# First-layer statistics moved into the products, the bias read in four transfers, W2 in halves, the first merge on VectorE

## The chip, the cores and the metric

One core of one Trainium2 chip runs the whole program in a single launch. The metric is the device time of that launch in microseconds, the median over repeated executions. TensorE (PE), VectorE (DVE), ScalarE (ACT), GpSimd (POOL) and the queues of SyncE (SP) work side by side; 16 DMA engines move data between HBM and the on-chip memory SBUF. Everything is float32.

## The reference, cut to what matters

```
def _gn(v, G=32, eps=1e-5):                 # group norm over (batch, channels, positions of one group)
    B_, H_, W_, C_ = v.shape
    g = v.reshape(B_, H_, W_, G, C_ // G)
    m = jnp.mean(g, axis=(1, 2, 4), keepdims=True)
    s = jnp.var(g, axis=(1, 2, 4), keepdims=True)
    return ((g - m) / jnp.sqrt(s + eps)).reshape(v.shape)

def conv(x, z, W1, b1, ..., W2, b2, Wb1, ..., Wb2, bb2):   # sizes: s 32, b 32, C 64, L 256, K 3, H 128
    h = relu(layernorm(z @ W1 + b1))
    w = (h @ W2 + b2).reshape(B, L, CI, CO, K)              # a convolution weight for every (b, l)
    hb = relu(layernorm(z @ Wb1 + bb1))
    bias = (hb @ Wb2 + bb2).transpose(0, 2, 1)
    x_uf = stack([pad(x)[..., i:i + L] for i in range(K)], -1)
    return einsum('sbilk,bliok->sbol', x_uf, w) + bias[None]

x = x + conv(_gn(x), layer 0 parameters)
x = x + conv(_gn(x), layer 1 parameters)
```

Each of the two layers normalizes x by group (32 groups of 8 positions), makes its own convolution weights from z by a small network, applies them, and adds a bias and the residual. The group statistics need all of the batch and all channels.

## The kernel before, in words

The work is cut into 128 chunks, numbered v = 0 to 127; 0 to 63 belong to layer 0 and 64 to 127 to layer 1. Chunk v is half h = v % 2 of the output channels of unit u = v // 2, and a unit is 4 batches and a quarter (64) of the positions. One iteration of the main loop, for chunk v, does this on TensorE: a first tile of weights of chunk v (`make`, L705 and L706: `h @ W2` for 8 output channels into PSUM, tiles `pg`, three buffers), then `products(v - 1)` (L760: the convolution of chunk v - 1 in four quarters, into PSUM tiles `pc`, two buffers), then eleven more weight tiles of chunk v. There are 672 matmul records in a chunk, 384 of the weights and 288 of the products.

- `take` (L717 on VectorE, L728 on ScalarE) adds b2 to a weight tile and writes it to `wall`, the weights of one chunk; `wall` has one buffer. One tile in three (kind 2) is split between VectorE and ScalarE; the others are VectorE's.
- In `products`, VectorE adds each quarter to the residual in `ring` (L772; `ring` has three slots, chunk v uses slot v % 3) and, in layer 0, takes the statistics of the result for layer 1 (`last_stats`, L369).
- GpSimd adds the bias to the residual ahead of time (`add_bias`, L653, from tile `bt`, one buffer) and normalizes the next unit's x (`normalize`, L691: one subtraction and one multiplication over half a unit, from `raw` into `xn`).
- SP issues nearly all DMAs in one queue, in program order: an issue that waits holds back all that follow it. In an iteration of the first 43 chunks these are: the store of the finished chunk (L658), `load_pieces` into `land` (L812), the next half unit into `raw` (L180), which waits until the subtraction of `normalize` has read the old one, the residual two chunks on (L202) and its bias (`load_bias`, L646). `load_bias` reads four rows of 8 KB and repeats each for 32 partitions, in one DMA of 1 MB.

The statistics of layer 0 are taken from x itself. Before chunk 0 only the first 11 of 32 groups are read (`first_phase`, loop over i; `needed` = 18 iterations give groups 0 to 8, which is what the first quarter of the positions needs); the other 21 groups are 168 pieces, four per chunk in chunks 1 to 42: `load_pieces(v)` at the start of iteration v fills `land`, and four VectorE instructions (`piece`, L819) placed among the weight tiles of the same iteration read it. Merges turn such statistics into mean and scale: `FirstMerge` before chunk 0, and eight `LaterMerge`s in later iterations, each with small DMAs through HBM (`turn`, `gather`, `root`; L445, L450, L471), small GpSimd operations (`mean`), a square root on ScalarE (L469) and a reciprocal on VectorE (L470). `Table.load` (L494) reads mean and scale back. `agenda(v)` says after which of the 12 weight tiles (todo[0] to todo[11]) each of these steps is issued.

## Time and profile before

| what | value |
|---|---|
| median of 3 runs | 4036.97 us (4033.2 to 4048.76) |
| the profiled execution, its own time | 4040.76 us |
| its span, first to last instruction | 4038.2 us |
| mean granted TensorE clock | 0.976 |

A profile is one execution. Busy times are sums for each engine; a wait is idle time of an engine just before an instruction, put down to what ended it. "x" is a count, times without a unit are microseconds, and a granted clock of 1.00 is 2.4 GHz, 0.50 is 1.2 GHz.

### The profile page before, as it was taken

What the parts mean: (1) busy time and instruction counts of PE and PEld (TensorE: products, weight loads), DVE (VectorE), ACT (ScalarE), POOL (GpSimd) and SP (SyncE); (2) the same over time, 40 slices, a digit from 0 to 9 for tenths busy, and PEclk for the clock granted to TensorE, in tenths of its full rate; (3) what the DMA queues carried; (4) which work ended last, traced back from release to release, by engine and by line L of the source; (5) the groups of instructions that cost most, each with busy time, mean ns of one, the idle gap of its engine ahead of it and who ended that gap; (6) DMA issues with size and microseconds to landing.
All of it is one profiled execution on the core that took longest, in us unless ns stands there. A gap on an engine that the chain in (4) does not pass through costs nothing.

```text
span 4038.2 us, 184843 instructions
## 1 busy us (share of the span) xinstructions
PE 3812.4 (94%) x86424; PEld 3699.1 (92%) x86424; DVE 2872.8 (71%) x3256; ACT 1263.0 (31%) x4330; POOL 1873.1 (46%) x713
## 2 busy tenths in 40 slices
PE   6888889989889989999999999999999999999999
PEld 4688889988888888999999999999999999999999
DVE  5766667766667666677677777777777777777776
ACT  4322222322233222333333233323332333333232
POOL 2144344444444444465454454555455454545453
PEclk8899999999999999999999999999999999999999
DMA  8844554545545454444446454555555555545453
GB/s 282 279 151 162 155 170 162 176 154 177 163 156 173 164 161 153 153 160 157 153 166 197 138 164 140 167 146 161 148 157 157 152 160 147 166 141 165 144 158 102
DMA packets 142861, 660.07 MB, mean 163 GB/s; under 512 B 45703, under 2 KB 51983, under 8 KB 76303
## 3 DMA queue, kind: packets, MB, share of 16 engines
q1 hardware_dynamic: 142095, 648.26, 51.0%
q8 instruction: 675, 11.06, 1.1%
q14 instruction: 91, 0.75, 0.1%
HBM read 499.16 MB, written 149.05 MB: 161 GB/s over the span
## 4 chain that ended last, share of the span: by engine, by line
PE 53%; DMA 1%; POOL 0%; issue 0%; ACT 0%; DVE 0%; SPq 0%; POOLq 0%; DVEq 0%
PE pg L705 35%; PE pc L760 14%; PE pg L706 4%; DMA bt<-bd 1%; DMA w2t<-in_L_conv_W_dram 1%; DMA land<-x 0%; POOL xn L691 0%; POOL ring L653 0%; ACT wall L728 0%; DVE wall L717 0%; ACT parts L390 0%; DVE ring L772 0%; DVE parts L369 0%; POOL four L454 0%; POOL found L455 0%
## 5 line engine op out<-in xcount | busy, mean ns | idle before, releaser
L705 PE MATMUL pg<-hT,w2t 128*64 128x128 f32 x24576 | 2779.2, 276 | 118.8 <-DVE wall L717 98.1
L705 PEld LDWEIGHTS pg<-hT,w2t 128*64 128x64 f32 x24576 | 2724.7, 139 | 156.2 <-DVE wall L717 112.5
L706 PE MATMUL pg<-hT,w2t 128*64 128x128 f32 x24576 | 2779.1, 276 | 3.5 <-issue 3.3
L706 PEld LDWEIGHTS pg<-hT,w2t 128*64 128x64 f32 x24576 | 2724.7, 139 | 7.6 <-issue 7.6
L717 DVE TENSOR_TENSOR wall<-pg,b 128x1024 f32<-128x1024 f32 (+1 forms) x1540 | 1871.8, 1218 | 600.3 <-PE pg L706 594.1
L728 ACT ACTIVATE wall<-pg,b 64x128 f32<-64x128 f32 x4064 | 1154.6, 468 | 2638.5 <-DVE wall L717 2638.3
L653 POOL TENSOR_TENSOR ring<-ring,bt 128x2048 f32<-128x2048 f32 x127 | 578.9, 4559 | 1934.0 <-DMA bt<-bd 1580.3
L760 PE MATMUL pc<-wall,xn 128*32 128x128 f32 (+1 forms) x36864 | 961.4, 264 | 60.4 <-DVE wall L717 31.6
L760 PEld LDWEIGHTS pc<-wall,xn 128*32 128x32 f32 x36864 | 925.4, 111 | 97.8 <-issue 89.8
L691 POOL TENSOR_TENSOR xn<-xn,tab 128x2112 f32<-128x2112 f32 x190 | 891.9, 4694 | 15.0
L772 DVE TENSOR_TENSOR ring<-pc,ring 128x512 f32<-128x512 f32 x512 | 353.9, 691 | 332.5 <-PE pc L760 224.5
L691 POOL TENSOR_TENSOR xn<-raw,tab 128x2112 f32<-128x2112 f32 x54 | 252.9, 4684 | 51.8 <-DMA raw<-in_xp_dram 51.5
L819 DVE BATCH_NORM_STATS2 first_parts<-land 128x6 f32<-128x512 f32 x168 | 114.4, 681 | 148.2 <-DMA land<-in_xg_dram 148.2
L369 DVE BATCH_NORM_STATS2 parts<-ring 128x6 f32<-128x256 f32 x512 | 191.9, 417 | 6.3
L209 DVE STREAM_TRANSPOSE xn<-raw 128x544 f32<-128x544 f32 (+1 forms) x128 | 138.9, 1104 | 0.0
L209 DVE STREAM_TRANSPOSE xn<-land 128x544 f32<-128x544 f32 (+1 forms) x128 | 138.8, 1103 | 0.0
L304 POOL TENSOR_TENSOR raw<-w2t,xn 128x256 f32<-128x256 f32 x16 | 10.3, 645 | 106.8 <-DVE xn L299 95.0
L328 PE MATMUL ph<-xn,wc 17*128 17x512 f32 x128 | 36.8, 776 | 16.3 <-DVE xn L294 6.8
L541 DVE BATCH_NORM_STATS2 first_parts<-ring 128x6 f32<-128x512 f32 x72 | 44.5, 676 | 9.3 <-DMA ring<-in_xg_dram 9.2
L328 PEld LDWEIGHTS ph<-xn,wc 17*128 17x128 f32 x128 | 10.1, 211 | 35.3 <-ACT xn L330 13.3
L330 ACT ACTIVATE xn<-ph,vec 128x1024 f32<-128x1024 f32 x32 | 36.1, 1199 | 5.4 <-DMA hd<-xn 3.2
L691 POOL TENSOR_TENSOR xn<-land,tab 128x2112 f32<-128x2112 f32 x8 | 37.6, 4702 | 0.0
(103 smaller groups left out, 366.3 us busy)
## 6 DMA issues: line engine op xcount, KB each, us to landing
bt<-bd SPq DMA_DIRECT2D x127, 1024.0 KB
ring<-in_xs_dram SPq DMA_DIRECT2D x64, 1024.0 KB
x<-ring SPq DMA_DIRECT2D x64, 1024.0 KB
ring<-x SPq DMA_DIRECT2D x64, 1024.0 KB
out_dram<-ring SPq DMA_DIRECT2D x64, 1024.0 KB
raw<-in_xp_dram SPq DMA_DIRECT2D x55, 1056.0 KB
land<-in_xg_dram SPq DMA_DIRECT2D x46, 1024.0 KB
raw<-x SPq DMA_DIRECT2D x128, 256.0 KB
```

The source lines that it names most:

```text
L209: nc.vector.transpose(xn[:, u % 2, k * NT // 2 + t, j0:j1], src)
L328: nc.tensor.matmul(p[:, r], self.w.wc[x, net], self.zq[x, net], start=True, stop=True)
L369: nc.vector.bn_stats(out, y[:, :, :, g * e : (g + 1) * e])
L653: nc.gpsimd.tensor_tensor(y, y, bts.pop(v).rearrange("p o (a m) -> p o a m", a=2), ALU.add)
L691: eng.tensor_tensor(o, i, tab[:, x, None, j0:j1].to_broadcast(list(o.shape)), op)
L705: nc.tensor.matmul(pg[0:C, k, :], w[:, k0 * C : (k0 + 1) * C], h0, start=True, stop=True)
L706: nc.tensor.matmul(pg[C:P, k, :], w[:, k1 * C : (k1 + 1) * C], h1, start=True, stop=True)
L717: nc.vector.tensor_tensor(place(rows, a), pg[rows].rearrange("p o (t m) -> p t m o", t=NT), b2[n][rows, kind, None, None, o0 : o0 + OG].to ...
L728: nc.scalar.activation(place(rows, a)[:, :, :, k], pg[rows, k].rearrange("p (t m) -> p t m", t=NT), AF.Identity, bias=b2[n][rows, kind, o0 ...
L760: nc.tensor.matmul(pc[t * S : (t + 1) * S, n0 - q * EB : n1 - q * EB, :], xn[:, u % 2, t, p, :], wall[:, t, a : a + (n1 - n0) * CH], start ...
L772: nc.vector.tensor_tensor(part, pc.rearrange("p (m a) o -> p a o m", a=2), part, ALU.add)
L819: nc.vector.bn_stats(first_parts[:, g, bg], lands[i % LAND])
```

## The change

1. The 168 pieces leave the weight tiles: `products(v)` now carries the four pieces of chunk v as its `turns` (two ahead of the first quarter's add, one behind it, one behind the second's), so data loaded in iteration v are read in iteration v + 1.
2. `load_bias` issues four DMAs of 32 partitions each instead of one of 128, for chunks up to 43; later chunks keep the one DMA.
3. `first_phase` ends after 18 iterations instead of 20. The four units of statistics that are left over (instead of two) run in iteration 1, and there the four kind-1 tiles go wholly to ScalarE. `FirstMerge` works on VectorE alone (`within`, `between`) and starts after iteration 17; the bias batches use other scratch memory.
4. In iteration 1 `products(0)` is issued ahead of the first weight tile of chunk 1.
5. The second half of W2 is loaded in four DMAs at the start; layer 1's W2 is loaded a half at a time, in iterations 63 and 64, instead of one eighth after each third tile of iterations 62 and 63.
6. `LaterMerge`: its DMAs and `Table.load` are issued by ScalarE's queue; one VectorE operation of `turn` becomes two small GpSimd operations; `gather` moves from the next iteration to todo[10] of its own, `mean` from todo[3] (behind `normalize` on GpSimd) to ahead of it, the square root from todo[10] to todo[5], the reciprocal to todo[6]. `Table.load` moves one iteration earlier, to todo[10].

The core of the diff:

```diff
@@ load_bias
-            nc.sync.dma_start(
-                out=bts[v].rearrange("p o l -> p (o l)"),
-                in_=bass.AP(src.tensor, src.offset, [src.ap[0], [0, S], src.ap[1]]),
-            )
+            to = bts[v].rearrange("p o l -> p (o l)")
+            n = 1 if v <= last_of[NQ - 1] + 1 else NT
+            for t in range(0, NT, n):
+                some = src[t : t + n]
+                nc.sync.dma_start(
+                    out=to[t * S : (t + n) * S],
+                    in_=bass.AP(some.tensor, some.offset, ([some.ap[0]] if n > 1 else []) + [[0, S], some.ap[1]]),
+                )
@@ products
-            turns = turns_of_half(u + 1, h, place_half(u + 1, h)) if UL <= u + 1 < U else []
+            if UL <= u + 1 < U:
+                turns = turns_of_half(u + 1, h, place_half(u + 1, h))
+            else:
+                turns = pieces_of(v)
@@ first_phase
-            for i in range(needed + 2):
+            for i in range(needed):
...
+                if i == needed - 1:
+                    merge = FirstMerge(first_parts.rearrange("p g b f -> p g (b f)")[:, 0:NG])
+                    table = Table(0)
+                    merge.within()
                 first_weights(i - (needed - 11))
-        rest = [lambda i=i, k=k: stats(i, range(k, k + 2)) for i in range(needed + 2, units) for k in (0, 2)]
+            merge.between()
+            biases(needed)
+            merge.root()
+            table.expand(nc.vector)
+            first_weights(11)
+            table.lay(table.spread(), [nc.vector.tensor_copy, nc.scalar.copy])
+            biases(needed + 1)
+            starting(0)
+            starting(1)
+        rest = [lambda i=i, k=k: stats(i, range(k, k + 2)) for i in range(needed, units) for k in (0, 2)]
@@ take
-                (add if alone else add_scalar)(slice(C, P), CH)
+                (add if v == 0 else add_scalar)(slice(C, P), CH)
-                add(slice(0, P), (3 * CH, 0)[kind])
+                (add_scalar if v == 1 and kind == 1 else add)(slice(0, P), (3 * CH, 0)[kind])
@@ agenda
-            w, r = divmod(v + 1, NH * BG)
+            w, r = divmod(v + 2, NH * BG)
-                todo[0].append(tables[w].load)
+                todo[10].append(tables[w].load)
+            for m in pending:
+                todo[0].append(m.mean)
+                todo[5].append(m.root)
+                todo[6].append(m.keep)
...
-            if v <= last_of[NQ - 1]:
-                for i in range(LAND):
-                    todo[8 + i if v == 1 else 5 + 2 * i].append(lambda i=(v - 1) * LAND + i: piece(i))
-            for m in pending:
-                todo[0].append(m.gather)
-                todo[3].append(m.mean)
-                todo[10].append(m.root)
+            n, i = divmod(v + 1, NH * UL)
+            if 0 < n < NL and i < NH:
+                for o in range(i * CH, (i + 1) * CH, OG):
+                    todo[1].append(lambda n=n, o=o: load_w2(n, o, o + OG))
...
                 todo[6].append(m.turn)
+                todo[7].append(m.send)
+                todo[10].append(m.gather)
@@ main loop
+            if v == 1:
+                products(0, cut_next)
             for k in range(len(order)):
                 pg = multiply(v, k)
-                if k == 0:
-                    products(v - 1, cut_next if v == 1 else None)
+                if k == 0 and v > 1:
+                    products(v - 1)
```

How the instructions stand on the engines, at the places that matter. First SP's queue in an iteration of about chunk 25, before (L658 stores a chunk, `land` takes the pieces, `raw` half a unit, `ring` a residual, `bt` its bias):

```order
L658 DMA x_12_84<-ring 128x2048
L812 DMA land<-in_xg_dram 128x2048
L180 DMA raw<-in_xp_dram 128x2112
L202 DMA ring<-in_xs_dram 128x2048
L646 DMA bt<-bd_160 128x1x2048
```

The same place with the change:

```order
L684 DMA x_12_84<-ring 128x2048
L834 DMA land<-in_xg_dram 128x2048
L180 DMA raw<-in_xp_dram 128x2112
L202 DMA ring<-in_xs_dram 128x2048
L672 DMA bt<-bd_160 32x2048 x4
```

Nothing moved in the queue; the bias, last in the row, is four DMAs of 32 partitions.

Second, VectorE from the products of one chunk (L772 adds a quarter, L369 takes layer 1's statistics) to the weight tiles behind them (L717), with the pieces (L819) before:

```order
L772 TENSOR_TENSOR ring<-pc,ring 128x64x8
L369 BN_STATS parts<-ring 128x6 x2
L772 TENSOR_TENSOR ring<-pc,ring 128x64x8
L717 TENSOR_TENSOR wall<-pg,b_0_219 128x128x8
L369 BN_STATS parts<-ring 128x6 x2
L717 TENSOR_TENSOR wall<-pg,b_0_219 64x128x8
L717 TENSOR_TENSOR wall<-pg,b_0_219 128x128x8 x2
L717 TENSOR_TENSOR wall<-pg,b_0_219 64x128x8
L717 TENSOR_TENSOR wall<-pg,b_0_219 128x128x8
L819 BN_STATS first_parts<-land 128x6
L717 TENSOR_TENSOR wall<-pg,b_0_219 128x128x8
```

The same stretch with the change, from the end of one chunk's tiles (L743 is now the add of `take`, L801 the add of a quarter, L843 a piece):

```order
L743 TENSOR_TENSOR wall<-pg,b_0_219 128x128x8 x2
L843 BN_STATS first_parts<-land 128x6 x2
L801 TENSOR_TENSOR ring<-pc,ring 128x64x8
L843 BN_STATS first_parts<-land 128x6
L369 BN_STATS parts<-ring 128x6 x2
L801 TENSOR_TENSOR ring<-pc,ring 128x64x8
L843 BN_STATS first_parts<-land 128x6
L369 BN_STATS parts<-ring 128x6 x2
L801 TENSOR_TENSOR ring<-pc,ring 128x64x8
L369 BN_STATS parts<-ring 128x6 x2
L801 TENSOR_TENSOR ring<-pc,ring 128x64x8
L743 TENSOR_TENSOR wall<-pg,b_0_219 128x128x8
```

The pieces left the tiles and stand between the adds of the first two quarters; the tiles behind follow each other with nothing between.

Third, SP's queue in iterations 62 and 63, where layer 1's W2 comes in (`w2t`), before:

```order
L136 DMA w2t<-in_L_conv_W_dram 128x1536
L202 DMA ring<-in_xs_dram 128x2048
L646 DMA bt<-bd_169 128x1x2048
L672 DMA xe_134<-rim 128x128
L136 DMA w2t<-in_L_conv_W_dram 128x1536 x3
L494 DMA spot<-tb_153 128x2x288
L658 DMA x_31_103<-ring 128x2048
L189 DMA land<-x_0_72 32x2x1024 x4
L136 DMA w2t<-in_L_conv_W_dram 128x1536
L202 DMA ring<-x_0_72 128x2048
L646 DMA bt<-bd_170 128x1x2048
L136 DMA w2t<-in_L_conv_W_dram 128x1536 x3
```

And with the change, iterations 63 and 64:

```order
L684 DMA x_31_103<-ring 128x2048
L189 DMA land<-x_0_72 32x2x1024 x4
L136 DMA w2t<-in_L_conv_W_dram 128x1536 x4
L202 DMA ring<-x_0_72 128x2048
L672 DMA bt<-bd_170 128x1x2048
L166 DMA edge<-xe_113 32x4x32 x2
L684 DMA x_31_103<-ring 128x2048
L189 DMA raw<-x_1_73 32x2x1024 x4
L136 DMA w2t<-in_L_conv_W_dram 128x1536 x4
L202 DMA ring<-x_0_72 128x2048
L672 DMA bt<-bd_170 128x1x2048
```

W2 is one iteration later, and all four DMAs of a half stand ahead of the residual and the bias; the table's load (`spot`) has left the queue.

## Rows read from the trace of the kernel before

**Rows 1.** The page: the span, and each engine's busy time with its share.

```profile
span 4038.2 us, 184843 instructions
PE 3812.4 (94%) x86424; PEld 3699.1 (92%) x86424; DVE 2872.8 (71%) x3256; ACT 1263.0 (31%) x4330; POOL 1873.1 (46%) x713
```

**Rows 2.** Windows: stretch, length, busy per engine, PEclk, DMA share, GB/s.

```profile
206.15:1643.72 1437.57, 1292.34 (x28897) 1254.85 (x28897) 976.02 (x1233) 416.97 (x1482) 625.86 (x213) 0.96 0.49 163
1674.60:2129.68 455.08, 453.39 (x10755) 448.29 (x10753) 326.02 (x390) 152.84 (x540) 232.70 (x80) 1.00 0.45 157
2158.04:2344.77 186.73, 173.86 (x4038) 170.84 (x4040) 135.94 (x146) 57.71 (x206) 93.64 (x47) 0.98 0.58 169
```

**Rows 3.** Chain that ended last, 1870 to 1935: start, length, what.

```profile
1875.16 7.18 PE pc L760 x288
...
1903.45 7.14 PE pc L760 x288
```

**Rows 4.** Waits, 206.15 to 1643.72: total, times, longest.

```profile
POOL ring L653 <- DMA bt<-bd: 579.4, 31, 21.9
...
DVE first_parts L819 <- DMA land<-in_xg_dram: 148.2, 34, 7.3
...
PE pg L705 <- DVE wall L717: 97.3, 50, 4.9
...
DVE found L470 <- ACT found L469: 27.5, 6, 6.8
```

**Rows 5.** Timeline, 401 to 436, of SP, POOL, DVE, PE (idle before).

```profile
401.06 0.53 SPq L646 DMA_DIRECT2D bt<-bd  x1
415.38 0.43 SPq L812 DMA_DIRECT2D land<-in_xg_dram  x1
425.50 4.51 POOL L653 TENSOR_TENSOR ring<-ring,bt 128x2048 f32<-128x2048 f32 x1 [20.34 <-DMA bt<-bd]
429.97 4.67 POOL L691 TENSOR_TENSOR xn<-raw,tab 128x2112 f32<-128x2112 f32 x1
429.85 0.69 DVE L819 BATCH_NORM_STATS2 first_parts<-land 128x6 f32<-128x512 f32 x1 [5.45 <-DMA land<-in_xg_dram]
431.72 0.47 PE L705 MATMUL pg<-hT,w2t 128*64 128x128 f32 x1 [3.35 <-DVE wall L717]
435.52 0.52 SPq L646 DMA_DIRECT2D bt<-bd  x1
```

**Rows 6.** Windows of 4 to 9 us, columns as in rows 2.

```profile
480.00:484.00 4.00, 4.00 (x160) 3.91 (x150) 3.19 (x7) 0.00 (x0) 0.00 (x0) 1.00 0.27 72
436.00:445.00 9.00, 9.00 (x228) 8.83 (x228) 5.57 (x8) 2.29 (x8) 3.54 (x2) 0.92 0.75 274
2873.00:2878.00 5.00, 5.00 (x97) 5.00 (x94) 3.42 (x4) 2.27 (x8) 4.92 (x2) 1.00 1.02 233
```

**Rows 7.** Timeline of SP, 2867 to 2873.

```profile
2867.80 3.74 SPq L189 DMA_DIRECT2D land<-x  x4
```

**Rows 8.** Groups by line and shape, DVE, 206.15 to 1643.72: busy, mean ns.

```profile
L369 DVE BATCH_NORM_STATS2 parts<-ring 128x6 f32<-128x256 f32 x344 | 129.1, 417 | 4.4
L772 DVE TENSOR_TENSOR ring<-pc,ring 128x512 f32<-128x512 f32 x172 | 118.9, 691 | 152.6 <-issue 84.4 <-PE pc L760 68.2
L819 DVE BATCH_NORM_STATS2 first_parts<-land 128x6 f32<-128x512 f32 x165 | 112.4, 681 | 148.2 <-DMA land<-in_xg_dram 148.2
```

**Rows 9.** Start: waits of PE, 140 to 182, and DVE's timeline.

```profile
PE pg L705 <- DMA w2t<-in_L_conv_W_dram: 4.9, 1, 4.9
...
157.92 2.47 DVE L541 BATCH_NORM_STATS2 first_parts<-ring 128x6 f32<-128x512 f32 x4
```

**Rows 10.** Timeline of POOL and ACT, 2195 to 2258.

```profile
2235.76 4.57 POOL L653 TENSOR_TENSOR ring<-ring,bt 128x2048 f32<-128x2048 f32 x1 [17.34 <-DMA bt<-bd]
...
2253.94 0.32 ACT L469 ACTIVATE found<-found,eps 8x32 f32<-8x32 f32 x1 [4.72 <-POOL found L455]
```

**Rows 11.** Waits of SP's queue, 206.15 to 1643.72.

```profile
SPq L494 <- DMA tb<-found: 28.7, 2, 15.1
```

More of the change, by code (lines that the diff above doesn't have):

```diff
@@ L264, in __init__ @@
             ht = [take(2 * BLK) for _ in range(2)]
-            self.bs = [take(BLK // 2).rearrange("p (t a m) -> p t a m", t=NT, a=2) for _ in range(4)]
             self.var = take(2 * NR * NR)
@@ L268, in __init__ @@
             self.ht = [[take(2 * BLK) for _ in range(2)], ht]
-            self.q = take(BLK)
+            self.q = raw[:, 2 * BLK : 3 * BLK]
             self.zq = take(2 * BLK).rearrange("p (n f) -> p n f", n=2)
+            self.bs = [take(BLK // 2).rearrange("p (t a m) -> p t a m", t=NT, a=2) for _ in range(4)]
         def form(self):
@@ L441, in turn, with send @@
         def turn(self):
[L442 to L443 removed]
             nc.vector.transpose(packed, pack.rearrange("p x g -> p (x g)"))
[L445 removed]
+        def send(self):
+            nc.scalar.dma_start(out=self.rows, in_=packed)
         def gather(self):
[L448 to L450 removed]
+            rows = self.rows.rearrange("(t x g) s -> x g t s", t=NT, x=4)
+            for x in range(3):
+                nc.scalar.dma_start(out=four[0 : self.n, x], in_=rows[x, 0 : self.n])
         def total(self, x, to):
@@ L458, in mean @@
             n, a = self.n, away[0 : self.n]
-            nc.gpsimd.tensor_copy(a, four[0:n, 0])
+            m, v, d = (four[0:n, x] for x in range(3))
+            nc.gpsimd.tensor_scalar(d, d, 1.0 / self.means.shape[2], None, ALU.mult)
+            nc.gpsimd.tensor_tensor(v, v, d, ALU.add)
+            nc.gpsimd.tensor_copy(a, m)
             self.total(0, found[0:n, 0])
@@ L707, in make, with take @@
             return pg
-        def take(pg, n, kind, o0, alone=False):
+        def take(pg, n, kind, o0, v):
             def place(rows, a):
@@ L815, in load_pieces, with pieces_of, piece @@
                 )
-        def piece(i):
-            j, bg, g = pieces[i]
-            nc.vector.bn_stats(first_parts[:, g, bg], lands[i % LAND])
+        def pieces_of(v):
+            def piece(i):
+                _, bg, g = pieces[i]
+                nc.vector.bn_stats(first_parts[:, g, bg], lands[i % LAND])
+            i = (v - 1) * LAND
+            return [lambda i=i: piece(i) for i in range(max(i, 0), min(i + LAND, len(pieces)))]
         def hidden_after(v):
```

109 lines of the change are left out of this document (48 added, 61 removed).

## The prediction

> **What bounds the kernel now.** I read the page first, then windows by stretch, then the waits, and last the timeline of one slow chunk. The page says TensorE: busy 94% of 4038.2 us, VectorE 71% [rows 1]. That share is a mean over stretches with different limits. Undisturbed, a chunk takes the distance of two products in the chain, 1903.45 - 1875.16 = 28.3 us, with TensorE never idle [rows 3]; 28.25 is where most late chunks stand, and I call it the floor. The windows say where the floor is missed. From products(1) at 206.15 to products(44) at 1643.72, 43 chunks (172 adds of four each [rows 8]), the mean is 1437.57 / 43 = 33.4 us, the granted clock 0.96 and the DMA share only 0.49. The next 16 chunks take 455.08 / 16 = 28.44 at clock 1.00 [rows 2]. So the first 43 chunks lose 43 x (33.4 - 28.25) = 223 us, and the six around the change of layer (186.73 us) lose 17. Nothing else of this size is left to win, since the floor itself is not touched.
>
> What do these 43 chunks wait for? By the waits, TensorE idles 97.3 us for VectorE's writing of `wall`, VectorE 148.2 us for the landing of `land` (34 times), and GpSimd 579.4 us for `bt` [rows 4]. GpSimd is less than half busy, so its wait looks harmless. The timeline shows that it is the cause [rows 5]. The bias is issued at 401.06, and GpSimd adds it at 425.50, 24.4 us later. Behind that add (4.51) stands the subtraction (4.67, ending at 434.64), which frees `raw`; only then can SP issue `raw`, and behind it in its queue the residual and the next bias, at 435.52. That is a closed loop of 24.4 + 4.5 + 4.7 + 0.9 = 34.5 us, above the floor. It reaches TensorE through the pieces: `land`, issued at 415.38, is there only at 429.85, just behind the bias; VectorE stands 5.45 us in front of the first piece, the weight tiles queue behind it, and TensorE idles 3.35 us until 431.72, where its matmul takes 0.47 us. What the gaps do not explain of the loss is the clock, 0.96 in this stretch.
>
> Why does 1 MB of bias take 24 us? While the bias alone is moving, the 16 DMA engines are 0.27 busy at 72 GB/s; with the loads of `raw` and `ring` in flight they move 274 GB/s at 0.75 [rows 6]. About four engines carry the bias, as many as its source has rows, and 1.05 MB / 72 GB/s is 14.6 us; the other 9.8 are the queue of `raw` and `ring` ahead of it. `land` and the store share those four engines and come behind it.
>
> **The change, term by term.**
>
> *Bias in four transfers.* I assume that 32 partitions are spread over all engines. The nearest rows are layer 1's loads of a half unit, four DMAs of 32 partitions (256 KB each) [rows 7]: in the window in which they are in flight the engines are 1.02 busy at 233 GB/s [rows 6]. At that rate the bias takes 4.5 us; the bound on the other side is today's 14.6. Ahead of it stand `raw` and `ring` as today, 9.8 us. The loop becomes 9.8 + 4.5 + 4.5 + 4.7 + 0.9 = 24.4 us, below the floor, and stops binding. Three more issues a chunk are about 0.5 us each on SP [rows 5] and hide in its waits. All five loads and stores of a chunk, 5.2 MB, need some 19 us at 274 GB/s, which fits into 28.
>
> *Pieces in the products.* Four times 0.68 us leave the tiles and go between the quarters' adds; their data were loaded an iteration earlier, so the 148.2 us of waits go. VectorE then has 4 x 0.69 of adds, 8 x 0.375 of statistics (129.1 / 344) and 4 x 0.68 of pieces, 8.5 us in a products stretch in which TensorE takes 7.14 [rows 3, 8]. But the first two pieces can run while the first quarter is multiplied, and TensorE needs the adds of the first two quarters alone before it goes on (two `pc` buffers): in order, these end about 2.8 and 4.9 us after the start, and TensorE wants the buffers at 3.6 and 5.4. I take no stall.
>
> *The 43 chunks.* I take 28.6 us each: the 28.44 of the next 16, plus 0.15 for a fuller DMA. 43 x 28.6 = 1230, against 1437.6: **-208 us**. Bounds: 28.3 (-221) and 30 (-148).
>
> *Start.* Eight statistics leave the merge (the last four are 2.47 us [rows 9]), about 5 us of VectorE; ScalarE's part of the merge becomes a few short VectorE operations. The 4.9 us that TensorE waited for W2's second half [rows 9] vanish from in front of products(0); against this, the tile that was made there, 1.75 us, now comes behind them. Iteration 1 gets eight more statistics (5 us) and loses four pieces (2.7) and four whole adds (4.9) on VectorE; its loads of the last two units stand behind a `raw` load in SP's queue, and VectorE may wait 2 to 4 us there. Net for products(1): **-4 us**, bounds -9 and +2.
>
> *Merges.* In six merges VectorE waits 27.5 us for the square root [rows 4]. ScalarE's queue now holds the small DMAs, and its `gather` must wait until `rows` has landed; behind it on ScalarE stand the tiles' halves, for which TensorE waits. The nearest wait for such a DMA is at most 15.1 us [rows 11]. From `send` to `gather` are three tiles, 5.3 us (a tile is (28.25 - 7.14) / 12 = 1.75), and ScalarE is missed only some 17 us after that: hidden. Whatever the 27.5 us give is in the 28.6.
>
> *Change of layer.* W2 comes an iteration later, all of a half ahead of a bias that is still one transfer on four engines. The square root of the last merge moves from tile 10 to tile 5, while GpSimd's `mean` follows that bias's add. Before, the add ended at 2240.33 and ScalarE got its input at 2253.94, behind 9.4 us of normalization and 4.2 us of small operations [rows 10]; now it would come at about 2245, where tile 5 stands near 2240: ScalarE and VectorE wait some 5 us, TensorE with its three buffers little. I take **-2 us**, bounds -10 and +8. Chunk 44 takes 1674.60 - 1643.72 = 30.9 us today [rows 2], 2.6 above the floor, in the wake of the loop: **-2**.
>
> *Sum.* -208 - 4 - 2 - 2 = -216 us on the span of 4038.2: 3822. The profiled execution's time is 2.6 us above its span and 3.8 above the median of the three runs, so I predict 3822 + 2.6 - 3.8 = **3821 us**.
>
> A rule speaks against the split: the Trainium skill, DMA: Bandwidth & Descriptors, section Bandwidth, asks to batch DMAs to 1 MiB or more, and its section Anatomy of one DMA, written for GpSimd's path, gives each DMA about 2 us of fixed cost. If the four paid that one after the other, 2.6 us each as an estimate from that page's fit, the bias would take 10.4 us, the loop 30.3, and the sum would be 3894 instead of 3821. The 233 GB/s of rows 6 speak against it: four such DMAs overlap. The Trainium skill's same page, section Why a DMA increments its semaphore by 16 and not by 1, says that a DMA runs on as many engines, up to 16, as divide the outermost dimension of both sides: four before, 16 now. The 0.27 of rows 6 agrees with four; that a source repeated 32 times is spread over 16, no run here shows yet.
>
> **The rivals.**
>
> *A. The products become VectorE's.* If the 8.5 us of VectorE set the length of the products instead of 7.14, each of 42 chunks pays 1.4 us: +59, 3880. For it: VectorE is at 68% in this stretch already. Against: the two buffers, worked out above.
>
> *B. The four transfers follow each other.* If they overlap so little that the bias takes 10 us, about midway between the 4.5 and the 14.6, the loop is 29.9 us and a chunk takes that instead of 28.6: +56, 3877. Against it, rows 6 and 7. The Trainium skill's fixed cost for each DMA (DMA: Bandwidth & Descriptors, Anatomy of one DMA) would make it come out so.
>
> *C. ScalarE's new waits are not hidden*, at the eight merges or in iteration 65: if half of 15.1 us shows eight times, +60, 3881.
>
> *D. The loop holds.* If the four transfers land as late as the one did, the loop stays at 34.5 us, the pieces' move only changes which engine waits, and the 43 chunks keep 33.4: 4037 - 8 = 4029, no change that can be told.
>
> *E. Slower.* If a 32-partition read of one repeated row ran on one engine, at 72 / 4 = 18 GB/s, and all four on the same one, the bias would take 58 us and the loop 58 + 19.9 = 78: +1900 us. It decides as soon as the bias takes longer than today's 14.6 us. Against it: layer 1's 32-partition loads fill all engines. No row shows the repeated source.
>
> **How the numbers follow.** Forecast 0.68 (own range 3795 to 3850), A 0.10, B 0.08, C 0.06, D 0.04, E 0.04. Half a percent (20 us) is about what a measurement of this kernel can tell from no change. Faster by more than that: forecast, A, B and C, 0.92; I give 0.91, the same 0.05, slower 0.04. The range 3790 to 3890 runs from the floor of 28.3 with the better bounds of the small terms to A, B and C, and leaves out D and E and the tails.
>
> **What would show it.** Right: 43 chunks between products(1) and products(44) in some 1230 us at clock 1.00; no wait of VectorE for `land`; GpSimd's wait for `bt` ending some 13 us after the issue of the bias; the DMA share near 0.6 there; products of 7.2 us in these chunks; products(0) some 5 us earlier. Wrong: a period near 30 with GpSimd's add still ending each `raw` wait (B), near 34 (D), products of 8.5 us (A), ScalarE idle in front of L451 or L456's successors (C). What I trust least is the change of layer, where two late loads meet a square root moved ahead. The sum stands or falls with the spread of the four transfers.

## The result, and the profile after

The changed kernel takes 3836.98 us (median of 4 runs, 3832.56 to 3847.03) against 4040.34 of the kernel before (4 runs); the ratio is 0.9499, 95% interval 0.9472 to 0.9527. The forecast was 3821 in a range of 3790 to 3890. The profiled execution took 3832.56 us. Its page answers to [rows 1]:

```profile
span 3829.7 us, 185123 instructions
PE 3745.1 (98%) x86420; PEld 3647.6 (95%) x86420; DVE 2847.4 (74%) x3251; ACT 1266.4 (33%) x4348; POOL 1883.2 (49%) x729
```

The windows between the same places as in [rows 2], products(1) to products(44) and the six chunks around the change of layer (columns as there):

```profile
205.70:1441.30 1235.60, 1226.16 (x28896) 1206.40 (x28896) 956.93 (x1228) 415.35 (x1482) 633.98 (x224) 1.00 0.58 189
...
1955.20:2135.90 180.70, 173.88 (x4035) 170.16 (x4032) 135.04 (x145) 57.54 (x206) 94.53 (x49) 0.99 0.59 181
```

Of the 208.5 us of span, 202.0 come from the 43 chunks, which take 1235.60 / 43 = 28.73 us each. Two parts are to be seen there: TensorE's idle time falls from 1437.57 - 1292.34 = 145.2 us to 9.4, and its busy time, for the same matmuls, from 1292.34 to 1226.16, with the granted clock at 1.00 instead of 0.96. The waits of this stretch, against [rows 4]:

```profile
POOL ring L679 <- DMA bt<-bd: 398.0, 29, 20.7
DVE wall L743 <- PE pg L732: 196.2, 382, 0.6
...
DVE ring L801 <- issue: 46.3, 33, 2.6
...
PE pc L789 <- issue: 8.3, 19, 0.7
```

The direction has turned: VectorE waits for TensorE (196.2 us, never over 0.6), TensorE no longer for VectorE's `wall`, and VectorE's wait for `land` is gone. GpSimd still waits 398 us for `bt`, which costs nothing now. The timeline of SP and GpSimd in one chunk shows why, against [rows 5]:

```profile
387.96 2.50 SPq L180 DMA_DIRECT2D raw<-in_xp_dram  x1
390.56 0.43 SPq L202 DMA_DIRECT2D ring<-in_xs_dram  x1
391.16 1.95 SPq L672 DMA_DIRECT2D bt<-bd  x4
...
378.37 4.60 POOL L679 TENSOR_TENSOR ring<-ring,bt 128x2048 f32<-128x2048 f32 x1 [14.29 <-DMA bt<-bd]
382.89 4.74 POOL L717 TENSOR_TENSOR xn<-raw,tab 128x2112 f32<-128x2112 f32 x1
387.71 4.70 POOL L717 TENSOR_TENSOR xn<-xn,tab 128x2112 f32<-128x2112 f32 x1
...
407.74 4.58 POOL L679 TENSOR_TENSOR ring<-ring,bt 128x2048 f32<-128x2048 f32 x1 [15.12 <-DMA bt<-bd]
```

From the bias's issue to its add are 16.6 us instead of 24.4 (medians over the chunks, worked out from the timelines: 16.2, against 22.8 before). With 4.6 for the add, 4.7 for the subtraction and 2.0 from `raw`'s issue to the bias's (median; 0.9 before) the loop is 27.5 us, about 1 us shorter than a chunk. So the subtraction is done (387.63) when `raw` is issued (387.96), if only just. SP's wait for the subtraction, ahead of `raw`, shows it for all 43 chunks; the first row is from the kernel before, the second from the changed one:

```profile
SPq L180 <- POOL xn L691: 676.4, 43, 20.1
```

```profile
SPq L180 <- POOL xn L717: 45.9, 10, 11.1
```

Before, each of the 43 issues of `raw` waited for the subtraction; now 10 do.

### The profile page after: what moved, and what is told of

Same layout as the page of the kernel before. It is cut to its first block, busy times and chain, and to the rows that moved or that the text cites. A ratio compares the mean times of both kernels' runs of the same rounds, so it can differ in the third digit from the quotient of the medians.

```text
span 3829.7 us, 185123 instructions
## 1 busy us (share of the span) xinstructions
PE 3745.1 (98%) x86420; PEld 3647.6 (95%) x86420; DVE 2847.4 (74%) x3251; ACT 1266.4 (33%) x4348; POOL 1883.2 (49%) x729
## 4 chain that ended last, share of the span: by engine, by line
PE 93%; DMA 3%; DVE 2%; POOL 1%; issue 1%; ACT 0%; SPq 0%; DVEq 0%; POOLq 0%; ACTq 0%
PE pg L731 62%; PE pc L789 24%; PE pg L732 7%; DVE wall L743 1%; DMA bt<-bd 1%; DMA hd<-xn 1%; POOL xn L717 0%; DMA wc<-in_L_conv_wc_dram 0%; POOL ring L679 0%; DMA raw<-in_xp_dram 0%; DMA w2t<-in_L_conv_z_dram 0%; DVE first_parts L553 0%; DMA land<-x 0%; DMA hT<-hd 0%; ACT xn L330 0%
## 5 line engine op out<-in xcount | busy, mean ns | idle before, releaser
L731 PE MATMUL pg<-hT,w2t 128*64 128x128 f32 x24576 | 2729.0, 274 | 15.3 <-DMA hT<-hd 5.2
L732 PE MATMUL pg<-hT,w2t 128*64 128x128 f32 x24576 | 2729.8, 274 | 0.7 <-issue 0.7
L731 PEld LDWEIGHTS pg<-hT,w2t 128*64 128x64 f32 x24576 | 2690.4, 137 | 36.8 <-issue 9.6
L732 PEld LDWEIGHTS pg<-hT,w2t 128*64 128x64 f32 x24576 | 2690.2, 137 | 3.5 <-issue 3.3
L743 DVE TENSOR_TENSOR wall<-pg,b 128x1024 f32<-128x1024 f32 (+1 forms) x1536 | 1874.2, 1220 | 667.5 <-PE pg L732 661.8
L789 PE MATMUL pc<-wall,xn 128*32 128x128 f32 (+1 forms) x36864 | 947.5, 262 | 23.9 <-issue 13.9
L789 PEld LDWEIGHTS pc<-wall,xn 128*32 128x32 f32 x36864 | 910.9, 110 | 62.6 <-issue 50.6
L717 POOL TENSOR_TENSOR xn<-xn,tab 128x2112 f32<-128x2112 f32 x190 | 892.1, 4695 | 15.0
L801 DVE TENSOR_TENSOR ring<-pc,ring 128x512 f32<-128x512 f32 x512 | 352.8, 689 | 260.5 <-PE pc L789 194.6
L717 POOL TENSOR_TENSOR xn<-raw,tab 128x2112 f32<-128x2112 f32 x54 | 254.2, 4707 | 39.3 <-DMA raw<-in_xp_dram 39.1
L369 DVE BATCH_NORM_STATS2 parts<-ring 128x6 f32<-128x256 f32 x512 | 190.6, 414 | 3.5
L843 DVE BATCH_NORM_STATS2 first_parts<-land 128x6 f32<-128x512 f32 x168 | 111.1, 682 | 0.0
L553 DVE BATCH_NORM_STATS2 first_parts<-ring 128x6 f32<-128x512 f32 x72 | 44.4, 677 | 13.4 <-DMA ring<-in_xg_dram 13.3
L328 PE MATMUL ph<-xn,wc 17*128 17x512 f32 x128 | 37.2, 782 | 16.6 <-DVE xn L294 7.7
L717 POOL TENSOR_TENSOR xn<-land,tab 128x2112 f32<-128x2112 f32 x8 | 37.6, 4706 | 0.0
```

The costliest lines, as they stand in the source:

```text
L328: nc.tensor.matmul(p[:, r], self.w.wc[x, net], self.zq[x, net], start=True, stop=True)
L369: nc.vector.bn_stats(out, y[:, :, :, g * e : (g + 1) * e])
L717: eng.tensor_tensor(o, i, tab[:, x, None, j0:j1].to_broadcast(list(o.shape)), op)
L731: nc.tensor.matmul(pg[0:C, k, :], w[:, k0 * C : (k0 + 1) * C], h0, start=True, stop=True)
L732: nc.tensor.matmul(pg[C:P, k, :], w[:, k1 * C : (k1 + 1) * C], h1, start=True, stop=True)
L743: nc.vector.tensor_tensor(place(rows, a), pg[rows].rearrange("p o (t m) -> p t m o", t=NT), b2[n][rows, kind, None, None, o0 : o0 + OG].to ...
```

## The experiments

All stretches are taken from the starts of products in each run's profile; "43 chunks" is products(1) to products(44).

| kernel | median us | ratio to before, 95% | 43 chunks | one |
|---|---|---|---|---|
| changed | 3836.98 | 0.9499 (0.9472 to 0.9527) | 1235.6 | 28.73 |
| one_bias | 4091.47 | 1.0142 (1.0107 to 1.0177) | 1482.3 | 34.47 |
| split_only | 3843.79 | 0.9521 (0.9499 to 0.9543) | 1238.3 | 28.80 |
| two_bias | 4494.77, one run | | 1862.3 | 43.31 |
| split_all | 3853.54 | 0.9546 (0.9517 to 0.9575) | 1233.5 | 28.69 |
| bias_first | 4019.59 | 0.9958 (0.9935 to 0.9981) | 1415.5 | 32.92 |
| both_first | 3851.87 | 0.9543 (0.9512 to 0.9575) | 1236.7 | 28.76 |
| eight_bias | 3881.09 | 0.9608 (0.957 to 0.9646) | 1288.3 | 29.96 |
| start_loads | 3835.37, one run | | 1238.3 | 28.80 |
| later_root | 3823.41, one run | | 1233.0 | 28.68 |
| both_first_split | 3835.79 | 0.9499 (0.9471 to 0.9526) | 1248.1 | 29.03 |
| last_root | 3822.60 | 0.9458 (0.9442 to 0.9475) | 1233.8 | 28.69 |

The theory was the loop: the bias's landing sets the period through add, subtraction and `raw`. Its first rival was that the pieces among the weight tiles were the cause, and that moving them was the cure.

### The change without the split, and the split without the change

one_bias, on the changed kernel:

```diff
-            n = 1 if v <= last_of[NQ - 1] + 1 else NT
+            n = NT
```

> The changed kernel with the bias in one transfer in all chunks; everything else of the change stays. Loop theory (the bias's landing closes a loop of bias, add, subtraction and raw, whichever engine shows the wait): in the kernel before, GpSimd's add starts 22.8 us behind the issue of the bias (median of 41 chunks), in the changed kernel 16.2; with the one transfer it goes back to about 23, the loop to 23 + 4.6 + 4.7 + 0.9 = 33 us, and 43 chunks at 33 to 34.5 take 1419 to 1484 us instead of the 1236 of the changed kernel: 4020 to 4085 us. VectorE shows no wait for land, and TensorE's wait goes to another place, the products, which need the late residual. Rival, pieces theory (the loss was VectorE's wait for land among the weight tiles, and moving the pieces cures it): the 43 chunks stay at 28.7 to 29.5 us, 3837 to 3870 us.

TensorE's waits in its 43 chunks:

```profile
PE pc L789 <- POOL xn L717: 78.8, 12, 12.9
PE pg L731 <- DVE wall L743: 40.8, 6, 9.0
PE pc L789 <- issue: 34.5, 25, 3.2
PE pc L789 <- POOL xn L720: 28.5, 6, 6.1
```

The loop is back at 34.47 us a chunk, and the whole is 51 us slower than before. VectorE hardly waits for `land` (8.8 us, twice); the time has gone to GpSimd's late normalization, 107 us of TensorE's waiting, a place that the kernel before did not show. So the wait for `land` was where the loop showed itself, not what it cost. The time is 6 us above the range, because the first iteration takes 54.8 us instead of 44.6, which was not foreseen; what makes it longer these runs do not show.

split_only, on the kernel before, has the new `load_bias` and nothing else.

```diff
-            nc.sync.dma_start(
-                out=bts[v].rearrange("p o l -> p (o l)"),
-                in_=bass.AP(src.tensor, src.offset, [src.ap[0], [0, S], src.ap[1]]),
-            )
+            n = 1 if v <= last_of[NQ - 1] + 1 else NT
+            for t in range(0, NT, n):
...
```

> The kernel before with the bias in four transfers of 32 partitions up to chunk 43, and nothing else of the change; the pieces stay among the weight tiles of the iteration that loads them. Loop theory: the loop falls to 16.2 + 4.6 + 4.7 + 1 = 26.5 us, below a chunk's 28.25; land is no longer behind a bias on four engines and lands some 8.5 us after its issue, about when the first piece is due; 43 chunks at 28.7 to 29.3 us, 1234 to 1260 instead of 1437.6: 3837 to 3863 us, VectorE's waits for land under 20 us in all (148.2 before). Pieces theory: VectorE still waits for land some 3 to 5 us in most chunks, the chunks stay above 31 us and the time above 3930 us.

Its window from products(1) to products(44):

```profile
212.40:1450.70 1238.30, 1226.79 (x28896) 1206.41 (x28897) 963.71 (x1233) 415.34 (x1482) 628.54 (x212) 1.00 0.58 188
```

It is the changed kernel's to within 3 us, with the pieces still among the weight tiles and no wait of VectorE for `land`. The split alone gives 3843.79, 97% of the gain; the other five parts of the change together give 7 us, which these runs can't tell from nothing.

### Opening the loop elsewhere, with the slow transfer kept

bias_first, on one_bias:

```diff
+            early = 1 < v <= last_of[NQ - 1]
+            if early:
+                todo[0].append(lambda: load_bias(v + 1))
             x, k = half_after(u + 1, h)
             if x < UL:
                 todo[0].append(lambda: load_half(x, k, place_half(x, k)))
...
-                todo[i].append(lambda: load_bias(v + 1))
+                if not early:
+                    todo[i].append(lambda: load_bias(v + 1))
```

> The changed kernel with the bias in one transfer again, as in one_bias, but for chunks 3 to 43 issued ahead of raw in SP's queue, so that it no longer waits for the subtraction. If the closed loop is the cause (and not the slow transfer in itself), it is opened at this place: the bias waits for GpSimd's add alone, the loop is 14.6 to 23 us + 4.6 + 0.9 = 20 to 28.5 us, below or at a chunk's 28.25, and the 43 chunks of 34.5 us in one_bias go to 28.3 to 29.5, 1217 to 1270 us. The first iteration keeps the 55 us that it took in one_bias (44.6 in the changed kernel): 3830 to 3885 us. Rival (a transfer on four engines that holds up what shares them is the cause, wherever it stands in the queue): chunks stay above 32 us, 3990 us or more.

It took 4019.59 us, 32.92 a chunk: by the numbers the rival's. The timeline of SP and GpSimd shows that the edit had not opened the loop:

```profile
605.42 0.33 SPq L180 DMA_DIRECT2D raw<-in_xp_dram  x1
605.80 1.45 SPq L202 DMA_DIRECT2D ring<-in_xs_dram  x1
...
596.20 4.55 POOL L679 TENSOR_TENSOR ring<-ring,bt 128x2048 f32<-128x2048 f32 x1 [19.89 <-DMA ring<-in_xs_dram]
600.70 4.69 POOL L717 TENSOR_TENSOR xn<-raw,tab 128x2112 f32<-128x2112 f32 x1
...
627.38 4.57 POOL L679 TENSOR_TENSOR ring<-ring,bt 128x2048 f32<-128x2048 f32 x1 [17.01 <-DMA ring<-in_xs_dram]
```

The add needs the residual as well as the bias, and the residual still stood behind `raw`, and so behind the subtraction: add, subtraction, `raw` at 605.42, residual, next add at 627.38 is a loop of 31.2 us. That the loop alone set the 32.92 us is not shown, though. The window of these 43 chunks, and TensorE's largest wait in it:

```profile
216.90:1632.40 1415.50, 1282.13 (x28900) 1250.65 (x28900) 960.83 (x1229) 416.83 (x1482) 632.53 (x224) 0.96 0.63 165
```

```profile
PE pc L789 <- issue: 117.9, 59, 7.0
```

Of the 1415.50 - 1282.13 = 133.4 us that TensorE idles, 4.4 are waits for GpSimd; most are waits put down to "issue", that is, to nothing that the profile shows (the last section says what they are). both_first, on bias_first, moves the residual too:

```diff
             if early:
+                todo[0].append(lambda: load_residual(v + 1))
                 todo[0].append(lambda: load_bias(v + 1))
...
```

> The changed kernel with the bias in one transfer, and for chunks 3 to 43 the residual and the bias both issued ahead of raw (bias_first left the residual behind raw, and its chunk of 32.9 us was a loop again: add 4.6, subtraction 4.7, raw's issue, residual 21 us behind it, and the next add). Loop theory: now both wait for GpSimd's add alone, the loop is 22.8 + 4.6 + 0.9 = 28.3 us at most, and with the bias still on four engines the 43 chunks take 28.3 to 30 us each, 1217 to 1290; with the 56 us of the first iteration 3830 to 3910 us. Rival (a transfer on four engines costs TensorE time by itself, through what shares these engines: in bias_first TensorE waited 118 us in its products for nothing that the profile names, 15 in the kernel before): these waits stay at 50 us or more, the chunks above 31 us, the time above 3950 us.

Its window, and the same two engines in one chunk:

```profile
218.60:1455.30 1236.70, 1225.76 (x28896) 1206.66 (x28896) 957.09 (x1229) 415.77 (x1482) 632.76 (x224) 1.00 0.61 188
```

```profile
604.56 0.53 SPq L672 DMA_DIRECT2D bt<-bd  x1
614.16 0.32 SPq L180 DMA_DIRECT2D raw<-in_xp_dram  x1
...
629.04 4.55 POOL L679 TENSOR_TENSOR ring<-ring,bt 128x2048 f32<-128x2048 f32 x1 [10.13 <-DMA bt<-bd]
```

The bias is one transfer again and as late as ever, 24.5 us from issue to add (median 24.0), yet the chunks take 28.76 us; one_bias, which differs in the order of the queue alone, took 34.47. That settles the cause: the slow landing costs time where it stands in a loop longer than a chunk, and here the loop is 24.0 + 4.6 = 28.6 us. TensorE idles 1236.70 - 1225.76 = 10.9 us, so four busy engines don't by themselves cost it time. Its busy time and clock are the changed kernel's too, so what the lower clock cost before belongs to the loop as well. The 15 us by which the total stands above the changed kernel lie mostly in the first iteration, 56.7 us, which is long in the changed kernel's variants with the bias in one transfer (54.8 in one_bias; 38.0 in the kernel before) and which the edit doesn't touch.

### How a transfer is spread

two_bias and eight_bias, on the changed kernel:

```diff
-            n = 1 if v <= last_of[NQ - 1] + 1 else NT
+            n = 2 if v <= last_of[NQ - 1] + 1 else NT
```

```diff
...
+            n = S // 2
+            for i in range(P // n):
+                some = src[i // 2 : i // 2 + 1]
+                nc.sync.dma_start(
+                    out=to[i * n : (i + 1) * n],
+                    in_=bass.AP(some.tensor, some.offset, [[0, n], some.ap[1]]),
+                )
```

> The changed kernel with the bias of the first chunks in two transfers of 64 partitions, each from two rows repeated 32 times, instead of four from one row each. Theory (a transfer runs on as many engines as its source has rows in the outermost dimension; in the trace of before the one transfer of four rows shows four completions, in the changed kernel each quarter shows 16): each half runs on two engines; if the two halves use different engines the bias takes what the one transfer took, GpSimd's add comes about 23 us behind the issue and the time is 4020 to 4085 us; if both use the same two, the 1.05 MB move at about 36 GB/s, half of the 72 of before, the bias takes some 29 us by itself, the loop is near 48 us and the time is near 3837 + 43 x 19 = 4650 us. Rival (the number of transfers in flight is what counts, not the shape of their source): the bias lands some 18 to 20 us after its issue, the loop stays near 29, and the time is 3840 to 3880 us.

> The changed kernel with the bias of the first 43 chunks in eight transfers of 16 partitions instead of four of 32. If the data and the queue ahead set the landing, GpSimd's add comes 16 to 18 us behind the first issue as with four (16.2), four more issues cost SP 2 us that hide, and the time is 3837 to 3855 us. If each transfer costs its 1.0 to 1.4 us whatever its size (the distance at which the four land in the changed kernel), the eight take some 5 us more, the add comes 21 us behind the issue, the loop is 31.3 us and the 43 chunks take 1346 us instead of 1236: 3945 us. If transfers of 16 partitions run on fewer engines than those of 32, above 4000 us.

In two_bias, the issue, the add, and a window in which only the bias was moving:

```profile
843.33 1.39 SPq L672 DMA_DIRECT2D bt<-bd  x2
...
874.29 4.49 POOL L679 TENSOR_TENSOR ring<-ring,bt 128x2048 f32<-128x2048 f32 x1 [27.11 <-DMA bt<-bd]
```

```profile
866.00:873.00 7.00, 0.43 (x4) 0.22 (x4) 0.00 (x0) 0.88 (x4) 0.00 (x0) 0.50 0.13 53
```

Two of 16 engines are busy (0.13), at 53 GB/s, some 26 for each instead of the 18 that the 72 of [rows 6] gave; so the two halves use the same two, one behind the other, as expected in kind, and the time is 4495 instead of 4650 because these engines are faster than reckoned. The median from issue to add is 32.3 us, the loop 32.3 + 4.6 + 4.7 + 0.9 = 42.5, the chunk 43.31. The Trainium skill, DMA: Bandwidth & Descriptors, section Why a DMA increments its semaphore by 16 and not by 1, says that a transfer takes as many engines as divide the outermost dimension on both sides, and of the 16 the lowest-numbered; the trace agrees with the number, and with two transfers that share their engines, but which of the 16 these are it does not show.

In eight_bias the add comes 17.3 us behind the first issue (median of 42 chunks), 1.1 later than with four: the 21 us that a cost paid for each transfer would have given are not seen, and each transfer of 16 partitions shows 16 completions, as those of 32 do. But its chunks take 29.96 us. Its window and TensorE's largest wait:

```profile
207.00:1495.30 1288.30, 1243.56 (x28896) 1218.46 (x28896) 958.58 (x1229) 415.44 (x1482) 632.51 (x224) 0.99 0.59 180
```

```profile
PE pc L795 <- issue: 36.2, 30, 4.0
```

None of the three expectations holds: the landing is right and the time is not. Of the 52.7 us more in the 43 chunks, 35 are TensorE's idle time and 17 its busy time at a clock of 0.99. The waits stand inside the products and are put down to nothing; split_all shows what they may be. SP's queue shows something else:

```profile
SPq L180 <- POOL xn L723: 135.8, 29, 19.7
...
SPq L678 <- DMA ring<-in_xs_dram: 170.6, 34, 5.9
```

The eight issues (L678) are spread over 13.0 us, against 1.7 for the four (medians). The expectation took them as 2 us that hide. In this trace the transfers take turns at eight semaphores, and an issue stands until the transfer that had the semaphore before it has landed: in one chunk the seventh stood until `raw` had landed (622.5) and the eighth until the first had (627.9). `raw` waits for the subtraction again in 29 of the 43 chunks (10 in the changed kernel): 17.3 + 4.6 + 4.7 and 1.3 from `raw`'s issue to the bias's are 27.9 us. Whether this queue or TensorE's own waits set the 29.96 is not shown.

### The change of layer, and the split everywhere

split_all, on the changed kernel, has `n = 1` for every chunk.

> The changed kernel with the bias in four transfers in all 127 chunks instead of the first 43. Theory of the change of layer (the one transfer of chunk 64's and 65's bias lands 15.8 to 17.7 us after its issue behind W2's loads, GpSimd's add ends at 2034.9, its small operations at 2039.6, and ScalarE's square root, moved to the fifth tile, waits 4.88 us, VectorE 4.10 behind it, TensorE 2.7): the add comes some 5 us earlier, the waits go, chunk 64 takes some 31 to 33 us instead of 36.1, the change of layer 3 to 5 us less; the other chunks, which are at 28.25 to 29.3 already, stay as they are: 3831 to 3836 us in place of 3837. Rival (the split loads more engines and collides with the loads of layer 1): chunks 68 to 127 get longer by 0.2 to 0.4 us each, 3845 to 3860 us.

First the changed kernel in chunk 64, which takes 36.1 us (timeline of POOL, ACT, DVE, and one of TensorE's waits in 1955 to 2136):

```profile
2030.31 4.57 POOL L679 TENSOR_TENSOR ring<-ring,bt 128x2048 f32<-128x2048 f32 x1 [14.81 <-DMA bt<-bd]
...
2039.58 0.32 ACT L478 ACTIVATE found<-found,eps 8x32 f32<-8x32 f32 x1 [4.88 <-POOL found L461]
...
2039.94 0.34 DVE L482 RECIPROCAL found<-found 8x32 f32<-8x32 f32 x1 [4.10 <-ACT found L478]
```

```profile
PE pg L731 <- DVE wall L743: 3.2, 2, 2.7
```

In split_all this chain is gone (the square root waits 0.03 us), but the chunk takes 36.0 us all the same, and chunk 63 33.8 instead of 29.2. TensorE's timeline, and the DMA queues (packets, MB, share of 16 engines) from 2018 to 2023:

```profile
2022.92 0.44 PE L789 MATMUL pc<-wall,xn 128*32 128x128 f32 x4 [4.81 <-issue]
```

```profile
q1 hardware_dynamic: 288, 1.00, 95.7%
...
q8 instruction: 1, 0.02, 1.6%
```

TensorE stops in the middle of a quarter for 4.81 us, and the profile names nothing that it waits for; one packet of its instruction queue arrives in that stretch, among engines 96% busy with data, and TensorE goes on behind it. And chunks 68 to 127 take 1699.8 us instead of 1679.6, as the rival had it, with more of such waits:

```profile
2135.30:3835.10 1699.80, 1682.80 (x39619) 1654.02 (x39619) 1265.40 (x1205) 534.60 (x1888) 852.48 (x315) 1.00 0.57 150
```

```profile
2135.90:3815.50 1679.60, 1673.18 (x39617) 1652.65 (x39616) 1262.28 (x1205) 534.87 (x1888) 849.53 (x315) 1.00 0.53 152
```

The first window is split_all's, the second the changed kernel's. Where no loop needs the faster landing, the split costs 0.34 us a chunk: half of the 20 us are idle time (17.0 against 6.4), half busy time.

later_root and last_root, on the changed kernel (the second moves only the merge of chunk 64):

```diff
-                todo[5].append(m.root)
-                todo[6].append(m.keep)
+                todo[8].append(m.root)
+                todo[9].append(m.keep)
```

```diff
+                todo[11 if v > NH * UL else 5].append(m.root)
+                todo[11 if v > NH * UL else 6].append(m.keep)
```

> The changed kernel with the later merges' square root at the eighth tile instead of the fifth and the reciprocal at the ninth instead of the sixth. Theory: ScalarE's wait of 4.88 us, VectorE's of 4.10 and TensorE's of 2.73 in chunk 64 go, since GpSimd's operations end 5.3 us (three tiles) before they are asked for; chunk 64 takes 33 us instead of 36.1, all other chunks stay, 3834 us. Rival (chunk 64 is long for the late products in its first part): it stays at 35 to 37 us.

> The changed kernel with one thing moved: the square root and the reciprocal of the merge that falls into chunk 64 come at the last tile. In later_root they came at the eighth, three tiles later than in the changed kernel, and TensorE still waited 3.8 us there, since GpSimd's add of that chunk came at 2027 and its small operations ended at 2036.4, 29 us after the products' start at 2007. If the late bias acts through the square root alone, the wait for wall goes, chunk 64 takes 31 to 33.5 us (32.6 in both_first_split) instead of 36.1, the six chunks around it 176 to 178 us instead of 180.7, and the time is 3831 to 3836 us, not to be told from the changed kernel. Rival (TensorE's late fetch of products and the late normalization make chunk 64 long): it stays at 35 to 37 us.

later_root: chunk 64 took 35.0 us. The wait moved three tiles on instead of vanishing, since the bias landed later still there (its add came 20.3 us behind the start of products(64), 16.9 in the changed kernel):

```profile
2036.83 0.34 DVE L482 RECIPROCAL found<-found 8x32 f32<-8x32 f32 x1 [4.55 <-ACT found L478]
```

last_root: the wait for `wall` is gone, chunk 64 takes 33.3 us and the six chunks 178.3. Its 3822.60 us is the lowest median of all, 14 us below the changed kernel's. The trace puts only 2.4 of these into the six chunks and spreads the rest over stretches that the edit doesn't touch; the two intervals still meet, so it is not shown to be faster than the changed kernel. One trace is a weak measure of chunk 64, too. start_loads (below) has the changed kernel's instructions there, but the add came 20.9 us behind the start of products(64); TensorE's wait for `wall`, in the six chunks, was

```profile
PE pg L731 <- DVE wall L743: 9.2, 2, 8.7
```

and chunk 64 took 40.9 us instead of 36.1. The chain from the late bias to TensorE is the same, and its price differs between the two traces.

both_first_split joins the order of both_first, the four transfers and this edit:

> The changed kernel with its four transfers, and with residual and bias ahead of raw for chunks 3 to 43; besides, the square root and the reciprocal of the one merge that falls into chunk 64 come at the last tile. If TensorE is the bound of these chunks and the landing no longer matters, they stay at 28.5 to 28.8 us; chunk 64 loses its wait of 2.7 us for wall: 3825 to 3837 us, not to be told from the changed kernel. Rival (raw, now last in the queue, lands late for the subtraction and closes another loop, raw, subtraction, multiplication): chunks of 29.5 us or more, 3860 us or more.

3835.79 us: chunk 64 took 32.6 us, the 43 chunks 29.03 each, 12.5 us longer in sum. The chunks lie between the two sides of the expectation, and the total can't be told from the changed kernel: a loop that is below a chunk is worth nothing more when it gets shorter.

### The start

start_loads, on the changed kernel:

```diff
-            todo[0].append(lambda: load_pieces(v))
+            late = 3 if v == 1 else 0
+            todo[late].append(lambda: load_pieces(v))
...
-                todo[0].append(lambda: load_half(x, k, place_half(x, k)))
+                todo[late].append(lambda: load_half(x, k, place_half(x, k)))
```

> The changed kernel with the loads of the pieces and of raw in the first iteration issued behind the load of the 20th unit instead of ahead of it. Theory of the start (of the 7 us by which products(0) came earlier the first iteration gives 6.6 back, 3.3 of it in VectorE's wait for that unit, whose load shares the engines with raw and land): the load lands 2 to 3 us earlier, VectorE's wait of 3.27 us falls under 1, products(1) comes 2 to 3 us earlier behind products(0), the first iteration takes some 42 us instead of 44.6, 3834 us. Rival (VectorE and ScalarE have more work there than TensorE, whatever waits): it stays at 44 to 45 us, and the wait appears elsewhere.

The first iteration still took 44.4 us, and VectorE's wait stayed:

```profile
DVE first_parts L553 <- DMA ring<-in_xg_dram: 3.8, 2, 2.8
```

The rival was right in the number. What the windows show is the clock. The changed kernel from 11 us ahead of products(0), then the kernel before from 9 us ahead of it:

```profile
150.00:161.10 11.10, 7.35 (x50) 4.62 (x50) 6.42 (x13) 3.99 (x9) 0.00 (x0) 0.72 1.01 408
161.10:170.00 8.90, 7.43 (x164) 6.58 (x168) 7.53 (x14) 0.00 (x0) 0.00 (x0) 0.58 0.98 294
178.00:205.70 27.70, 23.31 (x376) 21.55 (x371) 20.28 (x29) 18.67 (x66) 13.29 (x4) 0.94 0.72 259
```

```profile
159.00:168.10 9.10, 4.25 (x35) 3.33 (x33) 7.75 (x15) 2.18 (x4) 0.00 (x0) 0.52 1.03 361
168.10:177.00 8.90, 6.61 (x227) 5.72 (x224) 7.05 (x13) 0.00 (x0) 0.00 (x0) 1.00 0.43 154
```

Before, the stretch near the lower clock, 1.2 GHz, lay ahead of products(0), over a wait and one tile (TensorE busy 4.25 of 9.1 us), and products(0) had the full clock. Now products(0) itself runs in it, behind 11.1 us in which TensorE was busy for 7.35: 164 matmuls in 8.9 us instead of 227. The rest of the iteration stands at 0.94 instead of 1.00. In the whole iteration TensorE is busy for 37.12 us instead of 30.63, which is nearly all of the 6.6 us that it got longer; 1.75 of them are the tile that now comes behind products(0).

## Why the prediction was right

**Bias in four transfers.** The mechanism is shown by split_only and both_first. The size is off: in the chunk shown 11.6 us until the residual ahead of it has landed and 4.9 for the four, against 9.8 and 4.5; and from `raw`'s issue to the bias's are 2.0 us instead of 0.9. The loop is 27.5 us instead of 24.4: it no longer sets the period, but it has 1 us to spare and not 4, and in 10 of the 43 chunks `raw` still waits for the subtraction. Among the signs, "some 13 us" from issue to add was low even by the prediction's own sum (9.8 + 4.5 = 14.3). The rule weighed against the split, a fixed cost for each transfer paid one after the other, would have given 3894; eight_bias, with twice as many, lands only 1.1 us later.

**Pieces in the products.** "I take no stall" holds: in about half of the chunks the products take 7.21 us, and their mean, 7.64, is that of split_only, 7.62, which has no pieces in them. But the term's other half, that with the move the 148.2 us of waits go, is the step that misled: they go with the split alone, and without the split the move buys nothing (one_bias). Rival D had said just this of a loop that holds, at 33.4 us; it was 34.47.

**The 43 chunks.** 28.73 us against 28.6: -202 instead of -208. Of the 202, 66 are TensorE's shorter busy time at the clock of 1.00. This had no term of its own: it came in with the 28.44 of the later chunks, which stand at 1.00, and the prediction gave no reason why the first 43 would get that clock back. In 13 of the 43 the products are 0.8 to 1.8 us longer, in part by TensorE's unnamed waits.

**Start.** Forecast -4, measured -0.4, within the bounds. products(0) came 7.0 us earlier, and the first iteration took 44.6 us instead of 38.0. The step counted VectorE's work and waits, and not the stretch of low clock, which did not move with products(0).

**Merges, change of layer.** VectorE's 27.5 us at the square root in the 43 chunks are gone, and ScalarE's new waits cost nothing (C is out). The six chunks give -6.0 instead of -2: chunks 62 and 63, now free of W2's loads, give 6.3 back, chunks 65 to 67 2.5, and chunk 64 loses 2.8, by the late bias and the early square root that the step described, of which it wrote "TensorE with its three buffers little"; TensorE waited 2.7 us, and 8.7 in start_loads.

**Chunk 44.** It takes 28.25 us, -2.6 for -2; but the chunks up to 62 together are unchanged (513.9 against 514.3), so this term is nothing in sum.

**Sum.** The span fell by 208.5 us instead of 216. It is this near in part by luck: the start, chunk 44 and the 43 chunks gave less than forecast, the change of layer more, for a reason (W2's loads out of chunks 62 and 63) that its term had not priced.

**Rivals.** A and B did not happen; the longer products that A would have shown are there without the pieces too. E is answered by two_bias: a source of few rows does crowd on few engines, and a row repeated 32 times in its outermost dimension does not.

## What to carry to other kernels

An engine's idle time is free only as long as it doesn't stand in a closed loop: add up the landing, the operations behind it and the issue that they free, and compare the sum with the period. A wait that shows on another engine may be only where that loop comes to light, so taking that wait away moves it. The wait to look at is that of the issue which closes the loop: here `raw`, which stood in the queue for the subtraction in 43 of 43 chunks before and in 10 after. When cutting a transfer, look at its outermost dimension and at what else is then held up: the same cut that gave 200 us inside the loop cost 17 outside it.

## What the runs showed of the hardware that was not expected

TensorE's instructions come by DMA and can come late. The waits of TensorE that the profile puts down to "issue" stand mostly in the middle of the products. In the 43 chunks of the changed kernel, one_bias, split_only, split_all, bias_first, both_first and eight_bias every one of them ends 1.2 to 1.8 us behind the end of a packet of the instruction queue, of which there is one in 5.5 us. Their sums inside the products are 8.3 us in the changed kernel, 36.2 in eight_bias and 117.9 in bias_first. Two in one chunk of the changed kernel stand 128 matmuls apart, which with their weight loads are 256 instructions. The Trainium skill, Runtime: NRT & Kernel Launch, section Instruction fetch mechanics, says that instructions are refilled by DMA in blocks of 16 KiB and that this is mostly hidden; here it mostly is, at 8.3 us in 1236, and not in bias_first, at 117.9 in 1416.

The long waits come mostly with full DMA engines, the short ones do not. In the changed kernel, where none is over 0.7 us, the engines' share in the 3 us ahead of the late packet is 0.01 (median); in bias_first, where they reach 7.0, it is 1.01, and around the 4.81 us of split_all 96%. That the late packets stood behind data is argued from this; it was not tried by an experiment of its own, and what makes eight transfers worse than four stays open.
